# Layer 2's value products: reading the attention table in steps of 512 bytes instead of from a turned copy

## The chip, the cores and the metric

The kernel runs on one core of one Trainium2 chip. The metric is the device time of one launch in microseconds (us); less is better. The core's engines appear in the profile as PE (TensorE's matmuls), PEld (TensorE's weight loads), DVE (VectorE), ACT (ScalarE), POOL (GpSimd) and SP (SyncE, here a DMA issuer).

## The reference, cut to what matters

Four graph layers act in turn on `x` (128 batch entries x 64 nodes x 256 features, float32), each as `x = layernorm(x + layer(x))`. The change is in layer 2, an attention over 512 edges with 4 heads of 64 features:

```python
Xq = (H @ W_lin.T).reshape(bt, n, h, dh)
Xv = (H @ W_val.T).reshape(bt, n, h, dh)
e = einsum('behd,hd->beh', leaky_relu(Xq[:, src] + Xq[:, dst], 0.2), a) + log(A0[src, dst] + EPS)
attn = softmax of e over the edges of one source node
Y = segment_sum(attn * Xv[:, dst], src)     # per batch entry and head: a 64 x 64 matrix times Xv
return Y.reshape(bt, n, d) @ W_out.T
```

The kernel computes the segment sum as dense products: for each batch entry and head, a 64 x 64 matrix of attention weights times that head's 64 x 64 slice of `Xv`. That is 128 x 4 = 512 products.

## The kernel before

`X` stays in SBUF as 64 tiles; a tile holds two batch entries (index `b`), with 2 x 64 nodes on the 128 partitions and 256 features along each partition. Layer 2 takes two tiles (index `i`) a step, so it has 32 steps `k`. The steps form two halves of 16; `u_` is the step within its half.

- `scores` (L2070 to L2125) makes the edge scores. Its matmuls are L2054 (the maps), L2042 (transposes of `X`), L2091 (a node-to-edge product) and L2030 (the sum over a head's features, into 32 of the 128 PSUM partitions each).
- `softmax(half)` (L2127 to L2180) turns a half's scores into weights and scatters them with indirect DMAs into a table in DRAM, `attn_d[b]` (L2177).
- `fetch(half)` (L2182 to L2189) reads that table into `M2[half]`, a tile of 128 partitions x 64 x 128 floats, with eight DMAs, four on SP and four on POOL. A partition is (b, target node d). Along the partition stand the source nodes `n`, and for each `n` 128 columns `q`: 16 steps x 8. The eight columns of a step are (c, i, h): pair of heads, tile, head within the pair. So the 64 weights that a product needs on one partition, those of all `n` for one `q`, lie 128 floats, which is 512 bytes, apart. The trace's names drop digits, and `M2` is called `M` there.
- `load(k)` (L2191 to L2198) copies a step's 8 columns on ACT into the tile `mc` (two buffers) and turns them round, so that the 64 weights of a product are neighbours.
- `mapped(k)` (L2200) has POOL load the step's `Xv` from DRAM into `xr` (three buffers).
- `mixed` (L2205 to L2218) makes the step's 16 products (L2214). The stationary operand is the `xr` slice, 64 partitions x 64 columns; the moving operand is the 64 x 64 block of weights. Products of even and odd heads write PSUM partitions 0 to 63 and 64 to 127. An ACT copy (L2217) brings each `b`'s result to `yT`. Each float32 matmul of the source is two MATMUL records in the trace, each with its own weight load, so the 512 products are 1024 records. Such a record is called a pass below.
- `values` (L2220 to L2239) is the loop over the steps: the load of step k + 1, the products of step k, and the output product (L2237) with residual and norm statistics of step k - 1.

Layer 3 follows in blocks of four tiles, `blocks` (L2338), with matmuls L2302, L2312, L2320 and L2330; L2306 adds a constant on POOL and L2336 writes the output.

The order of the work is written by hand as a list of steps of these generators: seven steps of `values` go beside the last `scores` steps (L2283), six among softmax 1 and the first layer 3 blocks (L2349), then comes `fetch(1)` (L2350), and then

```python
            run(l3, val, l3, val, l3)
            run(*[val, val, l3] * 8, val, val, *[l3] * (NT // 4))
```

At build time the framework puts each engine's instructions into an order of its own, near the order of the source but not the same (the trace has the products of step 0 between the second and the third of eight L2091 passes); the first two copies of a half are held in source order (L2197). Each engine's queue runs in that order, and waits on semaphores are added where one engine needs another's result.

Of the kernel before, what the change touches and what calls it, by code (L numbers as in the profile page):

```python
# [8 lines left out]
F32 = mybir.dt.float32  # L9
# [6 lines left out]
N = 64  # L16
NB = 128
D = 256
P = 128
# [1285 lines left out]
def tile_adj_resnorm(ctx: ExitStack, tc: tile.TileContext, I: dict, out: bass.AP, layers: int = 4):  # L1305
    nc = tc.nc
    v, s, te = nc.vector, nc.scalar, nc.tensor
# [3 lines left out]
    def load(name, shape, src, eng=nc.sync, dtype=F32):  # L1311
        t = const.tile(shape, dtype, tag=name, name=name)
        eng.dma_start(t, src)
        return t
# [19 lines left out]
    wg0 = lh.tile([P, 2, D], F32, tag="wg0", name="wg0")  # L1334
    nc.sync.dma_start(wg0, kio(I["Wg0"]))
    ident = load("ident", [P, P], I["ident"], s)
    adj = load("adj", [N, N], I["adj"], s)
    wg1 = lh.tile([P, 2, D], F32, tag="wg1", name="wg1")
    nc.sync.dma_start(wg1, kio(I["Wg1"]))
# [216 lines left out]
    with tc.tile_pool(name="lw", bufs=1) as lw, tc.tile_pool(  # L1556
        name="l0c", bufs=1
    ) as lc, tc.tile_pool(name="l0p", bufs=2, space=PSUM) as pp, tc.tile_pool(
        name="l0r", bufs=1, space=PSUM
# [10 lines left out]
        def weights(p):  # L1570

            wi = lw.tile([P, 2, G], F32, tag="wi", name="wi", bufs=2)
            nc.sync.dma_start(wi, kio(I["WihT"][p - 1]))
            wh = None
            if p > 1:
                wh = lw.tile([P, 2, G], F32, tag="wh", name="wh")
                nc.sync.dma_start(wh, kio(I["WhhT"][p - 1]))
            return wi, wh
# [216 lines left out]
    lw, sm = own2(only1, name="l1w", bufs=1), own2(only1, name="l1s", bufs=2)  # L1795
# [108 lines left out]
    for q in range(NQ):  # L1904
        h = sm.tile([P, 4, 512], F32, tag="h", name="h")
# [72 lines left out]
    with ExitStack() as l2:  # L1978
# [27 lines left out]
        sc, M2 = [[None, None], [None, None]], [None, None]  # L2006
# [181 lines left out]
                        M2[half][b * N : (b + 1) * N, n0 : n0 + 16, :],  # L2188
                        attn_d[b][: N * N, :].rearrange("(d n) q -> d n q", n=N)[:, n0 : n0 + 16, :])  # L2189

        def load(k):  # L2191
            half, u_ = divmod(k, HU)
            m = sm.tile([P, 2, 2, 2, N], F32, tag="mc", name="mc")
            c = s.copy(m.rearrange("p c i h n -> p (c i h) n"),
                       M2[half][:, :, u_ * 8 : u_ * 8 + 8].rearrange("p n q -> p q n"))
            if u_ < 2:
                tc.keep_in_program_order(c)  # L2197
            return m  # L2198

        def mapped(k):  # L2200
            x = sm.tile([P, 2, D], F32, tag="xr", name="xr", bufs=3)
            nc.gpsimd.dma_start(x, xvd[k])
            return x

        def mixed(m, x):  # L2205

            yT = sm.tile([P, 2, 2, P], F32, tag="yT", name="yT")
            for b in range(2):
                r = slice(b * N, (b + 1) * N)
                py = pp.tile([P, 512], F32, tag="m", name="m")  # L2210
                for i in range(2):
                    for h in range(4):
                        o = i * P + (h // 2) * N
                        te.matmul(py[(h % 2) * N : (h % 2 + 1) * N, o : o + N],  # L2214
                                  x[r, i, h * N : (h + 1) * N], m[r, h // 2, i, h % 2, :],
                                  start=True, stop=True)
                s.copy(yT[:, :, :, r], py[:, :D].rearrange("p (i c n) -> p i c n", i=2, c=2))  # L2217
            return yT  # L2218

        def values():  # L2220

            K = NT // 2
            xr = [mapped(0), mapped(1)]
            m, yT = load(0), None
            for k in range(K + 1):
                y = yT
                if k < K:
                    if k < K - 2:
                        xr.append(mapped(k + 2))
                    mn = load(k + 1) if k < K - 1 else None  # L2230
                    yT = mixed(m, xr.pop(0))
                    m = mn
                if k:
                    po = scratch()
                    for i in range(2):
                        for c in range(2):
                            te.matmul(po[:, i * D : (i + 1) * D], y[:, i, c, :], wo[:, c, :], start=(c == 0), stop=(c == 1))  # L2237
                    ln.add(2 * (k - 1), po, 2)
                yield  # L2239
# [12 lines left out]
        lw, sm = own1(valuing, name="l2w", bufs=1), own1(valuing, name="l2s", bufs=2)  # L2252
        l3w = own1(valuing, name="l3w", bufs=1)
        ln = Norm(nc, sm, X, 4, act=True)
        val = values()
        w1 = l3w.tile([P, 2, P], F32, tag="w31", name="w31")
        nc.sync.dma_start(w1, kio(I["W31"]))
# [32 lines left out]
        with tc.tile_pool(name="l3s", bufs=2) as s3, tc.tile_pool(name="l3p", bufs=6, space=PSUM) as p3:  # L2290
# [4 lines left out]
            ag, h, uh = {}, {}, {}  # L2295
# [120 lines left out]
```

## Time and profile before

| what | value |
|---|---|
| median of 3 runs | 2255.51 us (2254.89 to 2256.37) |
| the profiled execution's own time | 2254.81 us |
| its span, first to last instruction | 2253.0 us |
| busy share of the span: PE, PEld, DVE, ACT, POOL | 98%, 53%, 80%, 42%, 7% |
| granted TensorE clock, mean | 0.994 |
| first and last L2214 pass start | 1987.1 us, 2215.9 us |
| ACT copies L2194, total | 34.7 us in 32 copies |

The span is 1.8 us shorter than the execution's time. PE's busy time counts an instruction from its start to a modelled end. Two passes that overlap in the array count once, so the pace of PE is read from the distances between starts and not from the mean duration of a pass. The stretch that the change touches runs from 1985 to 2217 us. What follows it is the last layer 3 blocks and the last output DMA.

### The profile page before, as it was taken

The numbers are of one execution on the slowest core, as the hardware profiler recorded it, in microseconds if no ns is written. First come the engines' busy times: TensorE is split into PE (matmuls) and PEld (weight loads), VectorE is DVE, ScalarE is ACT, GpSimd is POOL, SyncE is SP. The second block draws the span as 40 slices with busy tenths as digits, with TensorE's granted clock in tenths as the row PEclk, the third lists the DMA queues.
The fourth block names the chain that finished last, engine by engine and source line by source line (L and its number), as shares of the span: only waits on it lengthen the run. The fifth ranks groups of instructions, "written<-read, shape, count | busy, mean of one in ns | idle before, by whom it ended". The sixth has DMA issues, their size and how long they took to land. (4 is left out here: it accounts for less than half of the span.)

```text
span 2253.0 us, 29801 instructions
## 1 busy us (share of the span) xinstructions
PE 2197.9 (98%) x8746; PEld 1198.6 (53%) x8746; DVE 1808.5 (80%) x9217; ACT 952.3 (42%) x1746; POOL 161.7 (7%) x196
## 2 busy tenths in 40 slices
PE   8999999999999999999999999999999999999997
PEld 6445655445655445655444654554434333445987
DVE  5788887889888889888889998788947777657688
ACT  1432322433322343322343222434437876567675
POOL 0111111111000000000000000000000000100631
PEclk9999999999999999999999999999999999999999
DMA  7001010111010111010101000012210010221532
GB/s 233 22 19 38 1 39 1 38 38 57 1 38 1 38 38 57 1 38 1 38 38 56 1 19 19 20 54 98 74 54 24 29 42 24 77 74 43 151 90 80
DMA packets 44666, 101.53 MB, mean 45 GB/s; under 512 B 5297, under 2 KB 23857, under 8 KB 43217
## 3 DMA queue, kind: packets, MB, share of 16 engines
q1 hardware_dynamic: 38384, 84.64, 11.0%
q0 software_dynamic: 3984, 14.40, 2.3%
q8 instruction: 69, 1.13, 0.2%
q10 hardware_dynamic: 2128, 0.54, 0.1%
q14 instruction: 101, 0.82, 0.1%
HBM read 67.97 MB, written 31.59 MB: 44 GB/s over the span
## 5 line engine op out<-in xcount | busy, mean ns | idle before, releaser
L1669 PE MATMUL pq<-H,wi 128*128 128x512 f32 (+1 forms) x2016 | 812.6, 543 | 13.3 <-ACT gate L1696 7.0
L1696 ACT ACTIVATE gate<-pq,bl 128x512 f32<-128x512 f32 (+1 forms) x504 | 314.4, 631 | 610.6 <-PE pq L1674 497.8
L1669 PEld LDWEIGHTS pq<-H,wi 128*128 128x128 f32 x2016 | 377.2, 191 | 364.5 <-issue 281.1
L1674 PE MATMUL pq<-lh,wh 128*128 128x512 f32 (+1 forms) x1152 | 461.9, 528 | 0.9 <-DVE lh L1712 0.8
L1674 PEld LDWEIGHTS pq<-lh,wh 128*128 128x128 f32 x1152 | 218.1, 190 | 203.1 <-issue 144.2
L2097 DVE SCALAR_TENSOR_TENSOR xs<-xs 128x512 f32<-128x512 f32 x256 | 165.1, 685 | 70.1 <-ACT xs L2096 69.2
L1710 ACT ACTIVATE gate<-lc 128x512 f32<-128x512 f32 (+1 forms) x144 | 83.6, 580 | 276.4 <-DVE lc L1709 105.0
L2096 ACT COPY xs<-l 128x512 f32<-128x512 f32 x256 | 134.0, 596 | 53.9 <-PE l L2091 43.9
L2091 PE MATMUL l<-edge_s,xq 64*128 64x512 f32 x512 | 128.7, 616 | 0.4 <-ACT xs L2096 0.3
L2054 PE MATMUL m<-wqv,xT 128*128 128x512 f32 (+1 forms) x264 | 121.7, 597 | 2.8 <-DVE X L1279 1.9
L1913 PE MATMUL ps<-h,w 128*128 128x512 f32 x256 | 114.0, 603 | 3.2 <-ACT h L1907 3.2
L1298 ACT ACTIVATE X<-X,ln_sh,ln_rs 128x256 f32<-128x256 f32 x187 | 97.5, 592 | 40.7 <-DVE ln_sh L1294 31.2
L1860 PE MATMUL ps<-at,w 128*128 128x512 f32 x256 | 113.1, 593 | 0.0
L796 POOL PARTITION_ALL_REDUCE qQ<-qSG x62 | 73.5, 1186 | 512.6 <-DVE pc L134 291.1
L1282 DVE BATCH_NORM_STATS2 ln_st<-X 128x6 f32<-128x256 f32 x256 | 98.3, 414 | 1.5
L2054 PEld LDWEIGHTS m<-wqv,xT 128*128 128x128 f32 x264 | 46.4, 189 | 76.4 <-issue 36.1
L1913 PEld LDWEIGHTS ps<-h,w 128*128 128x128 f32 x256 | 48.6, 193 | 62.5 <-issue 53.2
L1860 PEld LDWEIGHTS ps<-at,w 128*128 128x128 f32 x256 | 47.2, 190 | 52.8 <-issue 51.9
L2091 PEld LDWEIGHTS l<-edge_s,xq 64*128 64x128 f32 x512 | 44.5, 186 | 56.9 <-issue 41.8
L1712 DVE TENSOR_TENSOR lh<-gate 128x512 f32<-128x512 f32 (+1 forms) x72 | 43.1, 602 | 33.7 <-ACT gate L1696 33.7
L130 DVE SCALAR_TENSOR_TENSOR CS<-GA,qE 64x1 f32<-64x1 f32 x294 | 61.7, 210 | 9.5
L130 DVE SCALAR_TENSOR_TENSOR GA<-qtg,CS,GA 64x1 f32<-64x1 f32 x294 | 61.6, 209 | 8.5
(611 smaller groups left out, 3277.1 us busy)
## 6 DMA issues: line engine op xcount, KB each, us to landing
wi<-in_WihT_dram SPq DMA_DIRECT2D x16, 1024.0 KB, 4.9
wh<-in_WhhT_dram SPq DMA_DIRECT2D x12, 1024.0 KB, 6.7
xd<-X SPq DMA_DIRECT2D x16, 512.0 KB, 2.6
X<-xd SPq DMA_DIRECT2D x16, 512.0 KB, 3.4
xv<-xv SPq DMA_DIRECT2D x32, 256.0 KB, 2.0
xr<-xv POOLq DMA_DIRECT2D x32, 256.0 KB, 3.0
X<-in_x_dram SPq DMA_DIRECT2D x15, 512.0 KB, 8.9
out_dram<-X SPq DMA_DIRECT2D x15, 512.0 KB, 2.9
```

Of the source, the lines that this page charges most:

```text
L130: self.nc.vector.scalar_tensor_tensor(o, a, s, b, op0, op1)
L1282: nc.vector.bn_stats(st, self.X[:, k, :])
L1298: nc.scalar.activation(x, x, AF.Identity, bias=sh[:, k : k + 1], scale=rs[:, k : k + 1])
L1669: te.matmul(ps, wi[:, kk, o * P : (o + 1) * P], at(kk, k), start=(kk == 0), stop=(k == 0 and kk == 1))
L1674: te.matmul(ahead[gt, c], wh[:, kk, o * P : (o + 1) * P], hst[:, kk, :M], start=False, stop=(kk == 1))
L1696: s.activation(gates[gt][:, c, :M], ps, AF.Tanh if gt == 2 else AF.Sigmoid, bias=bl[:, p - 1, o : o + 1])
L1860: te.matmul(ps, w1[:, k, c * P : (c + 1) * P], at[:, k, :], start=(k == 0), stop=(k == 1))
L1913: te.matmul(ys[c], w2[:, k, c * P : (c + 1) * P], h[:, k, :], start=(k == 2), stop=(k == 1))
L2054: te.matmul(pss[i][:, cols], xT[:, i, c, :], wqv[:, c, cols], start=(c == 0), stop=(c == 1))
L2091: mm = te.matmul(pl[:, b, :], xq[i][r, c * P : (c + 1) * P], GG[r, :], start=True, stop=True)
L2096: taken.setdefault(i, []).append(s.copy(x, pl[:, b, :]))
L2097: ready.append(v.scalar_tensor_tensor(x, x, 0.2, x, ALU.mult, ALU.max))
```

## The change

`load` is replaced by `weights`, which makes no instruction: it only describes the step's eight columns of `M2[half]` as (c, i, h, n). The products L2214 read their moving operand through that description, 64 floats per partition with a step of 512 bytes. The 32 ACT copies, the tile `mc` and the two program-order marks are gone. The products' shapes, their count, their stationary operand and their outputs stay as they were.

```diff
-        def load(k):
+        def weights(k):
             half, u_ = divmod(k, HU)
-            m = sm.tile([P, 2, 2, 2, N], F32, tag="mc", name="mc")
-            c = s.copy(m.rearrange("p c i h n -> p (c i h) n"),
-                       M2[half][:, :, u_ * 8 : u_ * 8 + 8].rearrange("p n q -> p q n"))
-            if u_ < 2:
-                tc.keep_in_program_order(c)
-            return m
+            return M2[half][:, :, u_ * 8 : u_ * 8 + 8].rearrange("p n (c i h) -> p c i h n", c=2, i=2)
...
-            m, yT = load(0), None
+            yT = None
...
-                    mn = load(k + 1) if k < K - 1 else None
-                    yT = mixed(m, xr.pop(0))
-                    m = mn
+                    yT = mixed(weights(k), xr.pop(0))
```

## The prediction, made before the result was known

> **What bounds the kernel now.** I read the page first (PE is busy 98% of the span), then the busy times in the stretch that holds all value steps, then PE's timeline there, then the waits. The stretch, with the columns length, PE, PEld, DVE, ACT and POOL busy, clock, DMA share and GB/s:
>
> ```profile
> 1985.00:2217.00 232.00, 229.27 (x2188) 172.29 (x2181) 163.77 (x490) 163.38 (x338) 64.82 (x97) 1.00 0.28 83
> ```
>
> PE lacks 2.73 us of being busy throughout; ACT, which makes the copies, has 69 us to spare. PE's timeline (start, length, engine, line, tiles, shape, count, idle before):
>
> ```profile
> 2008.72 1.92 PE L2030 MATMUL sc<-xs,az 128*32 128x512 f32 x16
> 2010.58 0.98 PE L2214 MATMUL m<-mc,xr 64*64 64x64 f32 x32
> ...
> 2125.74 1.06 PE L2312 MATMUL ps<-w,ag 128*128 128x128 f32 x8
> 2127.56 0.98 PE L2214 MATMUL m<-mc,xr 64*64 64x64 f32 x32 [0.76 <-ACT mc L2194]
> ...
> 2132.18 0.98 PE L2214 MATMUL m<-mc,xr 64*64 64x64 f32 x32
> 2133.08 1.99 PE L2237 MATMUL ps<-wo,yT 128*128 128x256 f32 x8
> ...
> 2137.74 1.95 PE L2302 MATMUL ps<-bda,X 128*128 128x128 f32 x16
> 2139.53 1.95 PE L2312 MATMUL ps<-w,ag 128*128 128x128 f32 x16
> ```
>
> From start to start, 16 L2302 passes of 128 columns take 1.79 us, which is 0.87 ns per moving column. Thirty-two L2214 passes of 64 columns take 0.90 us (2132.18 to 2133.08). One after the other at 0.87 ns they would take 1.78 us, so they run two side by side: 57 ns per pair, 16 pairs a step. Groups follow each other without a gap, except where the bracket names one. So the stretch is PE's stream of columns, and a nanosecond added to a pair is a nanosecond on the time.
>
> **What the change removes.** The tile's view of the copies:
>
> ```profile
> L2194 ACT COPY mc<-M x32: 1052/1089/1127, 1985.9 to 2204.7; 128x512 f32<-128x512 f32 x32
> ```
>
> They are 32 x 1.089 = 34.8 us of ACT, and nearly all of that lies beside PE's stream. PE's idle time that ends with a copy is 0.76 us (above, step 16, whose table half has just landed) and 0.22 us at step 0, by the timeline at 1987.09: 1.0 us together. I book -1.0 us. At step 16 the products then wait for the landing itself, at 2125.56 us by the chain of waits, while PE is in L2312 until about 2126.5, so nothing new is late there; queued behind that wait are L2312 and the rest of layer 3's stream. The first half's table was issued at 1958 to 1962 us, with at most 19.3 us to landing, before the first products at 1987. Other waits on ACT that a freer ACT could shorten (0.32 us on the copies L2096 at 2054.25; 0.23 us on `yT` in some steps) are inside the 2.73 us. That number is the most the stretch can give, if its passes keep their pace and their order; I book nothing of the rest.
>
> The other releases cost nothing. The second half's table has a tile in another pool, so holding the first half until its last products delays no DMA. POOL's `xr` loads wait for old products already (146.9 us in 25 waits); they land 3.0 us after issue and three buffers lie between, so later products only shift them. Behind them in POOL's queue stand L2306 and the table's DMAs, which PE's stream paces in the same way.
>
> **What it adds: the step of 512 bytes.** The 1024 passes now fetch each moving element 512 bytes from the last. No moving operand in this trace does so; layer 0's strided ones come in runs of 8 floats. The nearest rows are two.
>
> The first is PE's own other reader. Both lines L2042 and L1725 are single-pass transposes whose loaded operand has 128 columns; L2042 loads neighbours from `X`, L1725 loads floats 32 bytes apart from layer 0's `H`:
>
> ```profile
> L2042 PEld LDWEIGHTS m<-ident,X x128: 137/140/147, 1691.7 to 2032.3; 128*128 128x128 f32 x128
> ...
> L1725 PEld LDWEIGHTS pr<-ident,H x96: 186/190/196, 426.6 to 1217.1; 128*128 128x128 f32 x96
> ```
>
> The step adds 50 ns, 0.39 ns per column. Ordinary contiguous loads are 190 ns for 128 columns and 135 ns for 64, so 0.86 ns per column; the 190 ns of L1725 is that pace too, and L2042's is about 0.86 - 0.39 = 0.47. A step thus nearly doubles the time per column there, to 0.86 ns per element. A lone moving stream asks for no more than one element per 0.87 ns; a pair asks for two.
>
> The second row is ACT. Its contiguous copies, by shape, are 596 ns for 512 columns and 372 ns for 256, so 0.875 ns per column and 148 ns fixed. The strided copy is (1089 - 148) / 512 = 1.84 ns per column, 2.1 times as much.
>
> From these, four prices of a pair, 57 ns now:
> - each stream has a reader of its own at the weight loads' strided pace: 64 x 0.86 = 55 ns, nothing added;
> - the pair's two streams share one reader at that pace: 2 x 64 x 0.86 = 110 ns, +53;
> - each stream has its own reader, at ACT's strided pace: 64 x 1.84 = 118 ns, +61;
> - shared and at ACT's pace: 236 ns, +179.
>
> Below nothing I exclude a gain: contiguous passes of 128 and of 512 columns keep about the same pace per column, so a harder pattern has nothing to win. Against sharing speak the L2030 lines: 16 passes of 512 columns on the same 128 partitions take 1.86 us from start to start, four side by side. [...] Over 512 pairs: 512 x 53 ns = 27.1 us (61 ns: 31.2 us; 179 ns: 91.6 us).
>
> [...]
>
> **The sum.** -1.0 + 27.1 = +26.1 us on the profiled execution's 2254.81 us gives 2280.9. That execution lies 0.7 us under the median, so against the median of 2255.51 us it is 2281.6; I say 2281.5. PE's stream has nothing to hide the 27.1 us under: all 32 steps stand in the stretch. Only the 2.73 us of idle time could take some of it in.
>
> **Rivals.**
> 1. *The step is free* (first price). For it: one strided stream fits PE's strided pace, and the four streams of L2030 show that the array's inputs can be fed side by side. Against it: both rows of strided reading are about twice their contiguous neighbours. Time: 2255.5 less 1.0 to 2.7, so 2254.5 to 2252.8: not slower. This is the other side of my forecast; its place is the pair of passes at L2214 and it decides below 57 + 8.8 = 66 ns a pair, since 512 x 8.8 ns is 4.5 us, which is 0.2%, about what a measurement of this kernel can tell from no change.
> 2. *Both losses together* (fourth price): 2255.5 + 91.6 - 1.0 = 2346. For it: ACT's is the only row with this very step. Against it: ACT's pace doesn't fit PE's strided loads, less than half as long per column.
> 3. *A part of it*: a pair of passes with h and h + 1 reads neighbouring floats and may share fetches, or the streams interleave in part. 66 to 100 ns a pair is +4.6 to +22 us, so 2259 to 2277.
> 4. *The order changes*: without the copies the framework may order PE's and ACT's instructions in another way. For a gain over 4.5 us it would have to take time from outside the stretch too, since inside only 2.73 us are idle; the last blocks after 2217, with PE busy for 21.2 of the 33 us from 2220 on, are the one place. About 2250.
>
> That the copies stay in some form is no rival: the edit leaves no instruction that could make them. What it may fail to do is to free time on the engine that counts.
>
> **Chances.** Forecast (second or third price) 0.45; rival 1 0.30; rival 2 0.10; rival 3 0.09; rival 4 0.06. Faster: rival 4, 0.06. Same: rival 1, 0.30. Slower: 0.45 + 0.10 + 0.09 = 0.64. The range takes in rivals 1 and 3 and the forecast with the third price (2255.5 + 31.2 = 2286.7), 0.84 in all: 2252 to 2288. The forecast's own range is 2279 to 2288.
>
> **What would show it.** Right: starts of neighbouring L2214 groups show 1.75 to 1.9 us per 32 passes instead of 0.90, ACT's busy time falls by 34.7 us, the bracket at step 16 loses its copy, and all other PE groups keep their lengths. If 32 passes take 0.90 us, rival 1 holds and the sum is wrong at the price of the step. If they take 3.8 us, it is rival 2. If the pairs cost the same but the time moves by over 4.5 us, the order of PE's groups will have changed, and that view shows it.

## The result, and the profile after

The changed kernel takes 2282.07 us, the median of 4 runs (2281.22 to 2283.91), against 2255.28 us before (4 runs, 2254.89 to 2256.37). The ratio is 1.0118 with a 95% interval of 1.0106 to 1.013, so the change costs 26.8 us. The profiled execution has a span of 2280.6 us.

The stretch of the value steps, in the columns of the line shown for before (length, then PE, PEld, DVE, ACT and POOL busy), now runs to 2244 us:

```profile
1985.00:2244.00 259.00, 258.69 (x2194) 196.84 (x2187) 171.56 (x492) 138.40 (x306) 64.94 (x97) 1.00 0.26 74
```

It is 27 us longer. PE is idle for 0.31 us of it instead of 2.73, and ACT is 25 us less busy in it. PE's timeline at the same blocks as before (start, length, line, tiles, shape, count; the lines have moved by 5 to 7 numbers, so L2209 are the products, L2230 the output products, L2295 and L2305 layer 3's):

```profile
2127.02 1.95 PE L2305 MATMUL ps<-w,ag 128*128 128x128 f32 x16
2128.81 1.06 PE L2313 MATMUL ps<-bdah,h 128*128 128x128 f32 x8
2129.70 1.89 PE L2323 MATMUL ps<-w,uh 128*128 128x256 f32 x8
2131.52 1.94 PE L2209 MATMUL m<-M,xr 64*64 64x64 f32 x32
2133.39 1.99 PE L2230 MATMUL ps<-wo,yT 128*128 128x256 f32 x8
2135.32 1.94 PE L2209 MATMUL m<-M,xr 64*64 64x64 f32 x32
2137.19 1.99 PE L2230 MATMUL ps<-wo,yT 128*128 128x256 f32 x8
2139.02 1.95 PE L2295 MATMUL ps<-bda,X 128*128 128x128 f32 x16
```

From start to start, 32 product passes now take 1.87 us (2131.52 to 2133.39) where they took 0.90. The other groups keep their lengths, and the bracket at step 16, whose products start at 2135.32, is gone. They now stand ahead of a layer 3 block and not inside one, so the framework's order has changed there too. The last DMA of their half of the table landed 1.2 us before them (issued at 2114.7 us, 19.4 us to landing).

The distances between the starts of neighbouring PE passes, added up by line from the first product to the pass behind the last one, account for the whole difference:

| | before | after | difference |
|---|---|---|---|
| first product starts at | 1987.1 us | 1986.5 us | -0.6 |
| products | 31.8 us | 60.8 us | +29.0 |
| L2312 (with the wait for the copy of step 16) | 24.3 us | 23.3 us | -1.0 |
| all other passes | 172.8 us | 173.0 us | +0.2 |
| from there to the end of the span | 36.98 us | 36.93 us | -0.05 |
| span | 2253.0 us | 2280.6 us | +27.6 |

The first row holds two parts of opposite sign. The L2030 group ahead of step 0 starts at 1983.89 us before and at 1984.64 after, so this execution is 0.75 us late before anything that the change touches. Without that part the spans differ by 26.9 us, about as the medians do. Behind the L2030 group, step 0 gains 1.34 us. PE's timeline there, before and after:

```profile
1985.75 1.12 PE L2091 MATMUL l<-edge_s,xq 64*128 64x512 f32 x2
1987.09 0.98 PE L2214 MATMUL m<-mc,xr 64*64 64x64 f32 x32 [0.22 <-ACT mc L2194]
1987.99 1.98 PE L2091 MATMUL l<-edge_s,xq 64*128 64x512 f32 x6
```

```profile
1986.49 1.94 PE L2209 MATMUL m<-M,xr 64*64 64x64 f32 x32
1988.36 1.99 PE L2091 MATMUL l<-edge_s,xq 64*128 64x512 f32 x8
```

The wait for the copy is gone, and so are the two L2091 passes ahead of the products. The eight passes that now stand together take 1.92 us from start to start, no more than the six took before (1.91).

The products' pace alone would be 32 x (1.87 - 0.906) = 30.9 us. It shows as 29.0 mostly because the slower products also cover waits that before stood behind them: in five steps of the first half, PE waited 0.25 to 0.30 us for the copy to `yT` when the products were through, and now at most 0.01.

### The profile page after: what moved, and what is told of

It reads as the page before. It is cut to its first block, busy times and chain, and to the rows that moved or that the text cites. A ratio compares the mean times of both kernels' runs of the same rounds, so it can differ in the third digit from the quotient of the medians.

```text
span 2280.6 us, 29776 instructions
## 1 busy us (share of the span) xinstructions
PE 2228.3 (98%) x8746; PEld 1224.4 (54%) x8746; DVE 1815.4 (80%) x9217; ACT 928.1 (41%) x1714; POOL 162.0 (7%) x196
## 2 busy tenths in 40 slices
DMA packets 44665, 101.53 MB, mean 45 GB/s; under 512 B 5296, under 2 KB 23856, under 8 KB 43216
## 5 line engine op out<-in xcount | busy, mean ns | idle before, releaser
L2091 PE MATMUL l<-edge_s,xq 64*128 64x512 f32 x512 | 127.5, 616 | 0.4 <-ACT xs L2096 0.3
L1279 DVE TENSOR_TENSOR X<-ps,X 128x512 f32<-128x512 f32 x66 | 45.0, 681 | 38.6 <-PE ps L2230 33.7
L2091 PEld LDWEIGHTS l<-edge_s,xq 64*128 64x128 f32 x512 | 44.2, 186 | 56.2 <-issue 41.5
```

Of the source, the lines that this page charges most:

```text
L2091: mm = te.matmul(pl[:, b, :], xq[i][r, c * P : (c + 1) * P], GG[r, :], start=True, stop=True)
```

## The experiments

Each run is compared with the kernel before on the same chip. Its time is given with the ratio to that kernel and the 95% interval. The theory after the result was the prediction's: the step sets the price, PE's stream takes all of it, the copies were covered. Open was how a step slows a pass.

### Three shorter steps

The copies stay and only group the columns, so that the products' step is 4w bytes (w = 2, 4, 8):

```diff
-            m = sm.tile([P, 2, 2, 2, N], F32, tag="mc", name="mc")
-            c = s.copy(m.rearrange("p c i h n -> p (c i h) n"),
-                       M2[half][:, :, u_ * 8 : u_ * 8 + 8].rearrange("p n q -> p q n"))
+            m = sm.tile([P, 8 // w, N, w], F32, tag="mc", name="mc")
+            c = s.copy(m, M2[half][:, :, u_ * 8 : u_ * 8 + 8].rearrange("p n (g w) -> p g n w", w=w))
...
```

> The copies stay, but write pairs of neighbouring columns together, so that the products read their moving operand in steps of 8 bytes. Theory 'piece' (a stream loses when each element comes from another 16-byte piece of a partition, and the distance beyond that doesn't matter): two elements in a piece are enough, 32 product passes keep 0.9 us, time 2255 +-2 us. Rival 'distance' (the price grows with the step): a small price, 0.92 to 1.0 us per 32 passes, 2256 to 2259 us.

> The same with groups of four columns, so steps of 16 bytes. Theory 'piece': the whole price of the 512-byte step, 1.87 us per 32 passes, time 2281 to 2283 us (the copies are there still, so up to 1 us more than without them). Rival 'distance': a small part of it, below 1.2 us per 32 passes and below 2265 us.

> The same with all eight columns of a step together, so steps of 32 bytes. Theory 'piece': as with 16 bytes, 1.87 us per 32 passes, 2281 to 2283 us. Rival 'distance': between the 16-byte step and the 512-byte one, below 1.4 us per 32 passes and below 2272 us.

Measured: 8 bytes 2254.94 us, ratio 0.9996 (0.9987 to 1.0006); 16 bytes 2273.28 us, 1.0077 (1.006 to 1.0094); 32 bytes 2274.4 us, 1.0086 (1.0069 to 1.0102). PE's timeline, a product group and the start of what follows, first with 8 bytes, then with 16:

```profile
2191.37 0.98 PE L2213 MATMUL m<-mc,xr 64*64 64x64 f32 x32
2192.28 1.99 PE L2236 MATMUL ps<-wo,yT 128*128 128x256 f32 x8
```

```profile
2184.66 1.62 PE L2213 MATMUL m<-mc,xr 64*64 64x64 f32 x32
2186.21 1.99 PE L2236 MATMUL ps<-wo,yT 128*128 128x256 f32 x8
```

Thirty-two passes take 0.91 us with 8 bytes and 1.55 us with 16; with 32 bytes they take 1.57. So two floats in each 16 bytes were enough here, and one was not. Beyond that the distance hardly mattered up to 32 bytes, which speaks for 'piece' (the loss comes where each element is in another 16 bytes of a partition). But both theories missed the size: 16 bytes give two thirds of the 512-byte price (0.64 of 0.96 us per 32 passes), neither all of it nor a small part. Something is added between 32 and 512 bytes.

### A pass alone, and passes side by side

Extra matmuls behind the last block, on the kernel before (the kind sets the rows `r` and the stationary columns `c`, in one, two or four parts):

```diff
+            def probe(step, kind):
...
+                    tc.keep_in_program_order(te.matmul(
+                        ps[1 if r.start else 0][c, :M], ident[r, c], moving(r, step, t % 2 * 4),
+                        start=True, stop=True))
```

> The kernel before with extra matmuls behind the last layer 3 block, whose results nobody reads: groups of 8 matmuls (16 passes) with 64 stationary columns and 256 moving columns from the second half's table, first one pass at a time on all 128 partitions with steps of 4, 8, 12, 16, 32, 64 and 512 bytes, then pairs that write the two halves of PSUM's partitions from the same SBUF partitions (as in the products of one batch entry), pairs that read the two halves of SBUF's partitions, and all four quarters, each with steps of 4, 16 and 512 bytes. Theory 'shared' (the price on record as the second: the two streams of a pair share one reader): a pass alone takes 215 to 225 ns at every step, a pair from the same partitions takes 220 ns at 4 bytes and 440 ns at 512 bytes, a pair from different partitions stays at 220. Theory 'own' (the third price: each stream has its own reader, which a step slows): a pass alone takes 470 to 590 ns at 512 bytes, and a pair takes as long as a pass alone.

The busy times of three of its groups of 16 passes with 256 columns (length, PE, PEld, DVE, ACT, POOL busy, granted clock): alone at 4 bytes, alone at 512 bytes, and in pairs from the same partitions at 512 bytes.

```profile
2242.33:2245.83 3.50, 3.50 (x17) 2.24 (x17) 3.49 (x19) 2.38 (x6) 0.00 (x0) 1.00 0.10 31
2276.35:2282.66 6.31, 6.31 (x17) 2.34 (x17) 0.00 (x0) 0.00 (x0) 0.00 (x0) 1.00 0.00 0
2288.26:2292.19 3.93, 3.93 (x19) 1.61 (x15) 0.00 (x0) 0.00 (x0) 0.00 (x0) 1.00 0.00 0
```

By the distances between starts, a pass alone takes 216 ns at 4 bytes, 226 at 8, 341 at 12, 451 at 16, 460 at 32, 430 at 64 and 431 at 512. That is 0.84 ns per column without a step and 1.68 to 1.80 with a step of 16 bytes or more; the granted clock was 1.00 in all three lines. A pair at 512 bytes takes 432 ns, as long as one pass alone (the 3.93 us of the last line hold, besides, a first and a last pass without a partner); pairs from different partitions take 431 ns, and four passes from all four quarters 430 to 440. These are the values of 'own' and not of 'shared': a lone stream lost half its pace (431 ns against 216), and a second stream beside it cost nothing more (432). The names stand for these values; no trace shows a reader. For both 16 and 512 bytes the pace is alike (451 and 431 ns). So the step's length alone is not what is added between 32 and 512 bytes, at least when the two streams are 16 bytes apart as they were here.

### Pairs of 64 columns, and the place where two streams meet

The first probe has passes of the kernel's own size; the second varies the distance between the streams of a pair (64 partitions, output halves in turn):

```diff
+            def passes(step, offsets):
...
+                    at, c = offsets[t % len(offsets)], t % 2 * N
+                    tc.keep_in_program_order(te.matmul(
+                        o[c : c + N, :N], ident[:N, c : c + N], flat[:N, at : at + 63 * step + 1 : step],
+                        start=True, stop=True))
```

> The kernel before with extra products behind the last layer 3 block, 64 x 64 x 64 as the value products are and read by nobody: 32 passes each, alone with steps of 4, 8, 16 and 512 bytes; then in pairs that write the two halves of PSUM's partitions, with offsets 0 and 4 bytes and steps of 4 to 512 bytes (400 and 480 among them); pairs with 16, 32 and 256 bytes between their streams; last the eight columns of a step for both halves of the partitions, as the kernel has them. It asks why a pair of the changed kernel takes 146 ns where steps of 16 bytes give 118 ns. Theory 'same bank' (512 bytes, a power of two, brings every element and both streams to one place of the memory): pairs at 512 bytes take 146 ns, at 400 and 480 bytes 118 ns, and with another offset between the streams 512 bytes falls to 118 ns too. Theory 'company' (ACT, VectorE and DMAs beside the products slow the 512-byte reads): here, where they are nearly idle, all steps of 16 bytes and over give 115 to 120 ns, 512 among them, whatever the offset.

> The kernel before with extra products behind the last layer 3 block, read by nobody: groups of 32 passes in pairs on 64 partitions, as in the first probe of 64 columns, at a step of 512 bytes, with 4, 8, 12, 16, 20, 24, 28, 32, 48, 64 and 128 bytes between the two streams, then with their starts at 12 and 16 and at 4 and 16 bytes, then three orders of the eight columns of a step (the kernel's first), last the 4-byte distance with steps of 192, 256, 320, 384, 448 and 496 bytes. Theory 'piece' (two streams collide where they are in the same piece of 16 bytes): 4, 8 and 12 bytes take 146 ns a pair, 16 to 128 bytes and the two that cross a border at 16 take 112 ns; and the kernel's order would lie between, since half of its neighbours are in different pieces. Theory 'phase' (they collide unless their distance is a multiple of 16 bytes below 256): 4, 8, 12, 20, 24, 28 bytes and both border cases take 146 ns, 16, 32, 48, 64 and 128 take 112 ns, and all three orders take 146 ns. Both: of the last steps 256 bytes alone is slow, at 146 ns; the others take 112 to 120 ns.

In the first, a pass of 64 columns alone takes 58 ns at steps of 4 and 8 bytes, 116 at 16 and 111 at 512. With 4 bytes between the streams, a pair takes 147 ns at steps of 256 and 512 bytes, and 113 to 120 ns at 16, 32, 64, 128, 400 and 480. At 512 bytes, with 16 or 32 bytes between the streams, it takes 111 to 112 ns, and with 256 bytes 147 again. So the changed kernel's 146 ns go with the step and the distance of the two streams, and not with the company of other engines (in the second probe the kernel's order takes 146 ns with DVE, ACT and POOL busy for 0.00 us, the second line below). 'Same bank', as it was called, had these values, all but the one at 256 bytes' distance, where it gave 118 ns. That the streams meet in one place of the memory, no run shows.

In the second, at 512 bytes, distances of 4, 8 and 12 bytes take 146 to 147 ns and all others, up to 128 bytes and with both border cases, take 111 to 112. These are the values of 'piece': at this step two streams slowed each other where they were in the same 16 bytes, and (from the first of the two probes) where they were 256 bytes apart (147 ns). The kernel's order of columns takes 146 ns all along, though only half of its neighbours share a piece; an order with no such neighbours (0, 4, 2, 6, 1, 5, 3, 7) takes 111, but so does one with two of them in eight. 'Piece' expected the kernel's order to lie between; why half of the neighbours cost as much as all stays open. Among other steps at 4 bytes' distance, 256 bytes takes 147 ns, 496 bytes 118, and 192, 320 and 448 bytes 111 to 112. A step of 384 bytes takes 126, which neither theory gave.

These two probes are read with care, since the granted clock falls in them. The lines are three groups of the second: starts at 4 and 16 bytes (clock 0.50), the kernel's order (0.50), and a distance of 64 bytes (1.00):

```profile
2266.60:2268.38 1.78, 1.78 (x37) 1.78 (x35) 0.00 (x0) 0.00 (x0) 0.00 (x0) 0.50 0.03 9
2268.38:2270.71 2.33, 2.33 (x36) 2.33 (x34) 0.00 (x0) 0.00 (x0) 0.00 (x0) 0.50 0.00 0
2261.25:2263.04 1.79, 1.79 (x37) 1.79 (x34) 0.00 (x0) 0.00 (x0) 0.00 (x0) 1.00 0.00 0
```

The strided groups of 111 to 112 ns took 1.78 us for 32 passes at a clock of 0.50 and 1.79 us at 1.00, so the lower clock did not lengthen them. The contiguous pairs do not compare: at clock 0.50 they took 107 ns, where the kernel has 57 at 1.00.

### The step away from 512 bytes, in the changed kernel

```diff
-            M2[half] = lw.tile([P, N, P], F32, tag="M2", name="M2")
+            M2[half] = lw.tile([P, N, P + 4], F32, tag="M2", name="M2")
...
-                        M2[half][b * N : (b + 1) * N, n0 : n0 + 16, :],
+                        M2[half][b * N : (b + 1) * N, n0 : n0 + 16, :P],
```

> The changed kernel with four unused floats behind each source node's 128 columns in the table's tile, so that the products' step is 528 bytes and not 512. Theory 'two losses' (a stream whose every element is in another piece of 16 bytes goes at half pace, 64 columns in 111 to 118 ns; and where the step is a multiple of 256 bytes the two streams of a pair meet in one place of the memory, which makes 146 ns of it): 32 passes take 1.55 us as with steps of 16 bytes, not 1.87, and the time falls by 32 x 0.31 = 10 us to 2272 us. Rival (the long step costs by its length, or the pair collides because its streams are 4 bytes apart whatever the step): 1.87 us, 2282 us.

Measured: 2285.97 us (2282.82 to 2287.09), ratio 1.0126 (1.011 to 1.0141), where 'two losses' gave 2272. But the products did what it said. PE's timeline at step 16 and in a later step:

```profile
2142.91 1.72 PE L2209 MATMUL m<-M,xr 64*64 64x64 f32 x32 [6.60 <-DMA M<-attn_d]
2144.55 3.49 PE L2230 MATMUL ps<-wo,yT 128*128 128x256 f32 x8
...
2193.61 1.62 PE L2209 MATMUL m<-M,xr 64*64 64x64 f32 x32
2195.16 1.99 PE L2230 MATMUL ps<-wo,yT 128*128 128x256 f32 x8
```

Thirty-two passes take 1.55 us, and all products together 9.6 us less than in the changed kernel (51.2 instead of 60.8 us, added up as in the table). The time went to waits. The table's tile now takes pieces of 512 bytes with gaps between them (the profile counts 52857 DMA packets instead of 44665). A part of the table landed 23.9 us after its issue, where 19.4 was the longest in the changed kernel, and PE stood idle for 6.60 us until the half was there. Around this wait, from 2140.8 to 2147.6 us, the granted clock was 0.50, and the output products behind it took 3.49 us instead of 1.99. So the output products, which take in the wait, grew by 8.2 us in all.

This profile's first product also came 5.5 us later than the changed kernel's. About 0.9 us of that is there already at 1691 us, long before anything that the edit touches. The rest is another wait and the clock behind it, by PE's timeline ahead of step 0:

```profile
1986.00 0.66 PE L2042 MATMUL m<-ident,X 128*128 128x128 f32 x4 [2.81 <-ACT xv L2068]
1986.59 3.23 PE L2091 MATMUL l<-edge_s,xq 64*128 64x512 f32 x8
```

The copy L2068 had waited 3.64 us for a DMA of `xv`, while the DMA engines were busy for 0.97 of the time from 1976 to 1986 us (0.43 in the changed kernel). That the table's smaller pieces kept them busy is likely and not shown. The granted clock was 0.50 from 1987.2 to 1990.6 us, where the eight L2091 passes took 3.16 us from start to start instead of 1.92. So the second of the 'two losses' is shown in the kernel by the pace of its products (1.55 us per 32 passes at 528 bytes, 1.87 at 512), and the time tells nothing for it.

### The copies alone

The changed kernel with the copies put back, first unread, then read by two of the 16 products of a step (the last line of the cut is the second run's alone):

```diff
+            m = sm.tile([P, 2, 2, 2, N], F32, tag="mc", name="mc")
+            c = s.copy(m.rearrange("p c i h n -> p (c i h) n"),
+                       M2[half][:, :, u_ * 8 : u_ * 8 + 8].rearrange("p n q -> p q n"))
...
+                                  x[r, i, h * N : (h + 1) * N], (turned if i == h == 0 else m)[r, h // 2, i, h % 2, :],
```

> The changed kernel with the 32 ACT copies put back, whose results nobody reads: the products still read the table in steps of 512 bytes. The step alone, then, without the release of ACT. Theory on record: the copies cost 1.0 us where they stand in PE's way, of which nothing is left here since the products don't wait for them, so 2281 to 2284 us, the same as the changed kernel. Rival: ACT's 34.8 us are not covered, the copies delay the copies to yT and PE behind those, and the time is over 2286 us.

> The changed kernel with the 32 copies put back and read by two of a step's 16 products, so that they come one step ahead of their products and not all at once; the other 14 read the table in steps of 512 bytes. Theory on record (ACT's 34.8 us lie beside PE's stream): 14/16 of the products' 29 us are left, 25.4 us, and the copies' waits come back with up to 1 us: 2278 to 2283 us. Rival from the unread copies (2298 us: ACT's time counts where PE is held up longer): 2287 us or more.

The unread copies gave 2298.09 us, ratio 1.0192 (1.0176 to 1.0207), past the rival's bound. PE's timeline shows where:

```profile
1989.36 3.70 PE L2054 MATMUL m<-wqv,xT 128*128 128x512 f32 x8
1997.41 1.11 PE L2042 MATMUL m<-ident,X 128*128 128x128 f32 x4 [4.35 <-ACT xv L2068]
1998.46 3.79 PE L2091 MATMUL l<-edge_s,xq 64*128 64x512 f32 x8
...
2007.97 2.84 PE L2237 MATMUL m<-wo,yT 128*128 128x256 f32 x8 [2.00 <-ACT yT L2217]
```

With nobody to wait for, all 16 copies of the half stand in ACT's queue between 1986 and 2006 us, ahead of copies that PE needs. Around the first wait, from 1995.3 to 2002.1 us, the granted clock was 0.50, and the L2091 passes took 3.79 us instead of 1.99. The products kept 1.87 us per step. So this kernel measured an order of work and not the copies, and its loss is no evidence against the cover. Paced by readers, the copies gave 2278.0 us (2277.05 to 2283.15), ratio 1.0093 (1.0077 to 1.0108): at the lower edge of the 2278 to 2283 of the theory on record, and 9 us under the rival's 2287. ACT's 34.8 us lie beside PE's stream when they come step by step.

### The two batch entries in turn

In the changed kernel's trace, the second entry's first pair starts 0.59 us after the first entry's, just behind the start of the fifth of its eight pairs, and from there on the two run side by side. The edit lets them alternate from the start, in the changed kernel and in the kernel before:

```diff
-            for b in range(2):
-                r = slice(b * N, (b + 1) * N)
-                py = pp.tile([P, 512], F32, tag="m", name="m")
-                for i in range(2):
-                    for h in range(4):
-                        o = i * P + (h // 2) * N
...
+            pys = [pp.tile([P, 512], F32, tag="m", name="m") for _ in rows]
+            for i in range(2):
+                for h in range(4):
+                    o = i * P + (h // 2) * N
+                    for r, py in zip(rows, pys):
...
```

> The changed kernel with the products of the two batch entries in turn, not first all of one, then all of the other. In the changed kernel's trace a pair takes 146 ns, and the second entry's pairs start only when half of the first's are through. Theory 'own' (each stream is slowed by itself, whatever runs beside it): four streams keep 146 ns, 32 passes take 8 x 146 ns = 1.17 us, and the time falls by 32 x 0.7 = 22 us to 2260 us. Theory 'shared': the entries share nothing across their halves of the partitions either, so this order can't tell more than that; if all four streams share, 32 passes stay at 1.87 us and the time at 2282 us.

> The kernel before (copies, neighbouring floats) with the two batch entries' products in turn. If its pairs of 57 ns too run beside the other entry's, 32 passes take 8 x 57 = 0.46 us and the time falls by 32 x 0.45 = 14 us to 2241 us. Rival: the products of both entries now finish together, both PSUM tiles are held longer and the yT copies come one after the other behind them, so PE waits for these; then half of it or less is left, 2248 to 2256 us.

With the step of 512 bytes, 32 passes fell from 1.87 to 1.29 us, near the 1.17 of 'own', and the time to 2275.0 us, ratio 1.0088 (1.0072 to 1.0103): 7 us less than the changed kernel where 22 were expected. PE's timeline at step 16 and in a later step:

```profile
2136.86 1.66 PE L2209 MATMUL m<-M,xr 64*64 64x64 f32 x32 [5.01 <-issue]
2138.45 3.78 PE L2231 MATMUL ps<-wo,yT 128*128 128x256 f32 x8
...
2148.43 1.35 PE L2209 MATMUL m<-M,xr 64*64 64x64 f32 x32
2149.72 1.99 PE L2231 MATMUL ps<-wo,yT 128*128 128x256 f32 x8
```

The products, added up as in the table, take 17 us less. But PE stands idle for 5.0 us at step 16, until the table has landed (its last DMA at 2136.1 us; the bracket names none), and the granted clock was 0.50 from 2135.4 to 2142.3 us. The output products, which take this in, cost 6.8 us more, and L2091 5.3 us.

With the copies, 32 passes fell from 0.906 to 0.625 us, not to 0.46, and the time was 2253.72 us, ratio 0.9995 (0.9985 to 1.0004): nothing that these runs can tell. That is inside the rival's 2248 to 2256 us, but waits for the copies to `yT` come to only 0.5 us of it. PE's timeline of this kernel, in an early step and at step 16:

```profile
1997.12 0.69 PE L2214 MATMUL m<-mc,xr 64*64 64x64 f32 x32
1997.75 1.12 PE L2091 MATMUL l<-edge_s,xq 64*128 64x512 f32 x2
1998.80 1.99 PE L2238 MATMUL m<-wo,yT 128*128 128x256 f32 x8
2000.72 1.98 PE L2091 MATMUL l<-edge_s,xq 64*128 64x512 f32 x6
...
2128.57 0.69 PE L2214 MATMUL m<-mc,xr 64*64 64x64 f32 x32 [1.30 <-ACT mc L2194]
```

Of the gain of 9.6 us in the products, this profile keeps 3.5 us (a span of 2249.5 instead of 2253.0), and it is the fastest of the 11 executions. Most of the rest was given back in two ways. The framework's order now splits the eight L2091 passes into two and six in five more steps; the two take 1.05 us from start to start, and L2091 costs 5.3 us more in all. And at step 16 PE waits 1.30 us instead of 0.76, because the second half's table landed no earlier than before (2126.4 and 2125.7 us).

### The table fetched earlier

On top of the alternating products, in the kernel before. The edit moves the fetch by five entries of the list, where its expectation counts four:

```diff
-            run(sf, val, sf, val, sf, val, sf, val, sf, l3, l3, val, l3, val)
-            fetch(1)
-            run(l3, val, l3, val, l3)
+            run(sf, val, sf, val, sf, val, sf, val, sf)
+            fetch(1)
+            run(l3, l3, val, l3, val, l3, val, l3, val, l3)
```

> The kernel before with the two batch entries' products in turn, and with the second half's table fetched four entries of the hand-written list earlier. With the products in turn alone, 32 passes fell from 0.906 to 0.625 us, which is 9 us in 32 steps, but PE then stood idle for 1.3 us at step 16 until the table had landed and the profile's span fell by 3.5 us alone. Theory: the landing is what holds the rest back; fetched earlier by 2 us or more, it lets the time fall to 2246 to 2250 us. Rival: the table's scatter on POOL, not the place of the fetch in the list, sets the landing; then nothing moves, 2252 to 2254 us.

Measured: 2256.73 us, ratio 0.9997 (0.9988 to 1.0006). That is above the rival's 2252 to 2254 us, but so is the kernel before on this chip (2256.61). The rival holds in that nothing moved: the fetches again start behind the table's last scatter on POOL, which the trace has at 2104.5 us here and at 2102.1 us in the kernel before. No version beat the kernel before.

## Why the prediction was right, point by point

**The bound.** Right. The stretch was PE's stream of columns, and what the products gained in length went into the span, all but the waits that they now cover. The wait behind the products was 0.30 us at 0.91 us per 32 passes, 0.10 at 1.55 us (with copies at 16 bytes, without them at 528), and 0.01 at 1.87. So their length covers it, and not the freed ACT; the prediction had named these waits and booked nothing for them.

**The copies, -1.0 us.** Right in place, too small in size. At step 16, 1.0 us went where 0.76 had been booked, and at step 0, 1.34 us where 0.22 had been booked: 2.4 us together, with the framework's order changed in both places. So the measured terms are +29.0 - 2.4 + 0.2 = +26.8 us, where the sum on record has 27.1 - 1.0 = 26.1. The paced copies show ACT's 34.8 us under cover. The sign that was named for it, 34.7 us less busy time of ACT, didn't come: ACT's busy time over the whole span fell by 24.2 us (952.3 to 928.1). Added up one by one, ACT's instructions fell by 33.8 us; many overlap with their neighbours.

**The price of the step, +27.1 us.** The size was right (+29.0 us in the products, with 1.87 us per 32 passes inside the 1.75 to 1.9 that were named; by pace +30.9, nearer the third price's 31.2), but the step behind it failed: "the pair's two streams share one reader at that pace". A pass alone at 512 bytes took 431 ns instead of 216, and a pair 432, so a second stream added nothing, and no run shows a reader that two streams share. What spoke against sharing, the four L2030 streams side by side, was the better sign (four strided passes, from all four quarters, took 430 to 440 ns); the choice of the shared price was the author's estimate. The weight loads of L1725, 0.86 ns per strided element, were the wrong row to go by, though they belong to PE. A moving element took 1.68 to 1.80 ns at steps of 16 bytes or more, and the row that had it was ACT's with 1.84. The second and the third price, 110 and 118 ns, lay so close that the choice between them didn't show in the time.

**Two terms that weren't in the sum.** They nearly cancelled, and that the second price came so near is luck. A pair in the kernel takes 146 ns and not 111 to 118: its streams lie 4 bytes apart, and at a step of 512 bytes pairs 4 bytes apart took 146 to 147 ns in the probes too, pairs 16 bytes apart 111 to 112. What the two streams meet in is not shown. Sixteen such pairs one after the other would be 2.34 us. But the second batch entry's pairs, on the other 64 partitions, start while the first's last ones are still to come, which brings 16 pairs to 1.87 us, 117 ns each. By estimate, without the collision the kernel would have 1.55 us, as the products with 528 bytes had, and about 10 us less (32 x 0.32); without the overlap about 15 us more (32 x 0.47).

**Rival 1, the step is free.** It fell by its own point of decision, 66 ns a pair. What spoke for it, that one strided stream fits PE's strided pace, was the same weight-load row. **Rival 2** had the fourth price, 236 ns; since a second stream cost nothing more (432 ns against 431 alone), it didn't come. **Rival 3**, neighbouring floats that share fetches, had the sign wrong: at this step neighbours 4 bytes apart took 146 to 147 ns a pair, and streams 16 bytes apart 111 to 112. **Rival 4**, another order: the framework's order did change (step 0's products now stand ahead of all eight L2091 passes, step 16's ahead of a layer 3 block), worth no more than the 2.4 us above, waits for the copies included.

## What to carry to other kernels

Price a strided matmul operand by a pass of its own kind: here a float32 moving stream with one element per 16 bytes went at half pace, 1.7 to 1.8 instead of 0.84 ns per column, and with two elements per 16 bytes within 5% of full pace (226 against 216 ns a pass). Where a copy already turns data round on an engine with time to spare, grouping two columns is as good as turning them fully: the same product pace (0.91 us per 32 passes), with ACT copies of 648 instead of 1089 ns. Ask how much slack the next wait has before you speed up what stands ahead of it: in the changed kernel the table landed only 1.2 us ahead of step 16's products, and with the entries in turn PE lost 5.0 us there. When two errors can cancel, as the collision and the overlap did here, a right total proves no step; measure one pass alone.

## What the runs showed of the hardware that was not expected

- Two strided streams in the same 16 bytes of a partition slowed each other at a step of 512 bytes: at distances of 4, 8 and 12 bytes a pair of 64 columns took 146 to 147 ns, at 16 to 128 bytes 111 to 112. At a step of 256 bytes, a distance of 4 bytes took 147 ns as well.
- Strided pairs took 111 ns at a granted clock of 0.50 as at 1.00.
- ACT's copy of 512 columns gained from runs of two floats as PE's stream did: 1089 ns with single floats 512 bytes apart, 648 ns with runs of 8 bytes, 621 and 622 ns with runs of 16 and 32 bytes.
- Passes on the upper 64 partitions, issued behind 16 passes on the lower 64, began only when ten of those had started (0.59 us after the first, in the changed kernel); alternated, 32 contiguous passes took 0.625 instead of 0.906 us.
- Three waits of PE cost more than their length: at or just behind waits of 2.81, 5.01 and 6.60 us the granted clock was 0.50 for 3.4, 6.8 and 6.8 us, and the groups behind them took 3.16 us instead of 1.92 (L2091), 3.78 and 3.49 instead of 1.99 (output products). No such fall stood at waits of 0.76 and 1.30 us, nor at one of 2.30 us in the kernel before (to 1320.05 us; clock 1.00 in the 6 us after it). What sets it is not shown: the profile of the paced copies has one (1991.9 to 1998.7 us) without a wait of PE over 1 us.
